# A hand-made instruction order for a transformer layer: its planner gets other durations, hand-over times and constants of choice

## The chip, the cores and the metric

The kernel runs on one core of one Trainium2 chip. A core has four engines that compute, each with its own instruction queue that is worked off in order: TensorE (PE in the profile; its weight loads are listed as PEld), VectorE (DVE), ScalarE (ACT) and GpSimd (POOL). SyncE (SP) issues DMA transfers. Engines wait for each other by semaphores. The metric is the device time of one execution in microseconds, the median of several runs.

## The reference

One layer of a transformer with pre-normalisation, on x of 2 x 2048 x 256 in float32: causal attention with 16 heads of 16 columns and rotary positions, then a gated feed-forward network of width 704 whose activations and weights are rounded to a 4-bit grid (FP4) in blocks of 16.

```python
def _L0_attn_ref(x, Wq, bq, Wk, bk, Wv, bv, Wo, bo):
    q = split_heads(x @ Wq.T + bq)
    k = split_heads(x @ Wk.T + bk)
    v = split_heads(x @ Wv.T + bv)
    q, k = (rope(q), rope(k))
    att = jnp.einsum('bhqd,bhkd->bhqk', q, k) / math.sqrt(HEAD_D)
    att = jnp.where(mask, att, -jnp.inf)          # lower triangle
    att = jax.nn.softmax(att, axis=-1)
    y = jnp.einsum('bhqk,bhkd->bhqd', att, v)
    return y.transpose(0, 2, 1, 3).reshape(b, t, N_EMBD) @ Wo.T + bo

def _L0_ffn_ref(x, w_gate, w_up, w_down):
    gate = fp4_linear(x, w_gate)                  # both operands through FP4
    y = fp4_linear(x, w_up)
    h = jax.nn.silu(gate) * y
    return fp4_linear(h, w_down)

x = L0_attn_x
x = x + _L0_attn_ref(_layernorm(x, axis=-1), ...)
x = x + _L0_ffn_ref(_layernorm(x, axis=-1), ...)
```

## The kernel before

**The work.** Each of the two sequences is cut into four chunks of 512 positions (c = 0 to 3), and the 16 heads into four groups of four. For a chunk and a group there are two passes over the keys up to the diagonal. The first computes scores with the queries on the partitions (`max_steps`, tile `sc`, line 900) and takes their row maxima on VectorE (line 924). The maxima are split into three bfloat16 parts (lines 958 and 961), transposed on TensorE (line 974) and copied to `mT` (line 980). The second pass (`value_steps`) computes scores with the keys on the partitions into tile `sx`: line 1017 puts minus the maximum there, line 1025 adds the product, line 869 the mask on the diagonal. ScalarE takes the exponential into `ex` (line 1040), and line 1070 multiplies it with the values into `av`. After the last key, `av` is copied, transposed and divided (lines 1092, 1104, 1114, 1118). Beside this run the projections of the next chunk (`project_steps`, `pj` line 701, `pv` line 819), the FP4 rounding of the weights (`weight_items`), and the output projection and feed-forward network of finished chunks (`ffn_steps`; `po` line 1225, `pg` line 1276, `pd` line 1359, transposes in line 1151).

**Three tilings.** TensorE is used in three ways: score products on two strips of 64 rows ("strip"), value products on column tiles of 32 ("value"), and everything else with the whole array ("whole").

**The order.** The program is straight-line, and its order on every engine is decided while it is built. Each step adds tasks to a `Plan` (lines 110 to 151) with `add(engine, cost, run, reads, writes, due, ...)`: `cost` is a duration in us that the programmer supplies, `due` a place on a scale of urgency. That scale (lines 1417 to 1427) gives each slot, a chunk and group, 0.4 (c+1) units for its first pass and 0.6 (c+1) for the second pass of the slot before, 80 units in all. `Plan.ordered` (lines 153 to 243) then plays the program through as a list scheduler: it keeps, for each engine, the time at which it is free, and for each task the time at which what it reads is ready. Again and again it takes the engine whose next task can start first, and among that engine's tasks that can start within PATIENCE of it the one with the smallest due. A task of TensorE with another tiling than the one before has CHANGE added to its due in that comparison, and pays ENTER in time once taken. Tasks due more than AHEAD after the oldest outstanding due aren't looked at. FEED_M and FEED_V are taken off the due of the score tasks, and TURN, in slots, puts off the second pass. HOP is the time from a task's end until a task on another engine can start on its result. Buffers are counted too: ROOM allows three `ps` tiles in PSUM (shared by `sc`, `sx`, `pj` and `pg`), four `ex` tiles, one `pm`, and so on; a task that needs a new one can't start before the last user of an old one has ended (`vacancy`, line 168). The order found is the order in which instructions are issued; the chip then runs them by semaphores, and the planned times have no other effect on it.

Of the kernel before, what the change touches and what calls it, by code (L numbers as in the profile page):

```python
# [66 lines left out]
AHEAD = 2.0  # L67
CHANGE = 0.02
FEED_M = 0.3
FEED_V = 0.3  # L70
PATIENCE = 0.15
TURN = 0.25
# [15 lines left out]
HOP = {PE: 0.235, DVE: 0.09, ACT: 0.09, POOL: 0.09, SP: 0.05}  # L88

ENTER = dict(strip=0.17, value=0.11, whole=0.12)  # L90
# [15 lines left out]
class Task:  # L106
    __slots__ = "engine cost run due tiling feeds left ready end after new".split()


class Plan:  # L110
# [7 lines left out]
    def add(  # L118
        self, engine, cost, run, reads=(), writes=(), due=0.0, books=(), tiling="whole", feeds=0.0
# [3 lines left out]
        t.tiling, t.feeds = tiling, feeds  # L123
# [29 lines left out]
    def ordered(self):  # L153
# [14 lines left out]
        def vacancy(kind):  # L168
# [5 lines left out]
            for thing in held:  # L174
                if all(u.end is not None for u in thing.users):
                    at = max(u.end + HOP[u.engine] for u in thing.users)
                    if best is None or at < best[0]:
                        best = at, thing
            return best

        while len(out) < len(self.tasks):
# [4 lines left out]
            for e, some in waiting.items():  # L186
# [3 lines left out]
                for due, n, t in some:  # L190
# [3 lines left out]
                    for thing in t.new:  # L194
                        if thing.kind not in vacant:
                            vacant[thing.kind] = vacancy(thing.kind)
# [23 lines left out]
            for thing in t.new:  # L220
                held = rooms[thing.kind]
                if len(held) == ROOM[thing.kind]:
                    held.remove(vacancy(thing.kind)[1])
# [13 lines left out]
            for a in t.after:  # L237
                a.left -= 1
                a.ready = max(a.ready, t.end + (HOP[e] if a.engine != e or e == SP else 0.0))
# [6 lines left out]
def on_scalar(n):  # L246
    return 0.2 + 0.833e-3 * n


def on_vector(n):  # L250
    return 0.178 + 1.042e-3 * n


def on_pool(n):
    return 0.12 + 2.3e-3 * n


def product(n):

    return max(n / 600, 0.28) + 0.01  # L260
# [7 lines left out]
def layer_kernel(  # L268
# [156 lines left out]
    def deviation(pool, kind, src, thing, due):  # L425
# [17 lines left out]
        add(DVE, 0.66, stats, [thing], [dev], due)  # L443
# [3 lines left out]
    def normed(dst, src, got, things, due):  # L447
# [4 lines left out]
        add(DVE, 0.46, run, *things, due)  # L452

    def fp4(src, thing, r, n, engine=POOL, step_of=None):
# [6 lines left out]
        by_block = 0.09 + 1.88e-3 * n if engine == POOL else on_vector(n)  # L461
# [7 lines left out]
        def scaled(due):  # L469
# [17 lines left out]
            add(DVE, on_vector(n) + 0.64, sizes, [thing], [small16], due)  # L487
            add(POOL, 0.24, nudged, [small16], [small16], due)
            add(engine, by_block, divided, [small16], [thing], due)

        def rounded(due):
# [24 lines left out]
            add(DVE, 2 * (0.18 + 0.55e-3 * n), powers, [thing], [step], due)  # L516
# [17 lines left out]
    def transpose_plain(raw, thing, put, target, due):  # L534
# [11 lines left out]
        add(PE, 0.57, turn, [thing, fixed], [pm], due)  # L546
# [9 lines left out]
    def load_rounded(w, row, rows, col, cols, put, target):  # L556
# [12 lines left out]
        def turn(due):  # L569
# [11 lines left out]
            add(PE, 0.3, run, [raw, fixed], [pm], due)  # L581
            add(ACT, 0.45, lambda: put(st["pt"]), [pm], [target], due)
# [39 lines left out]
    def norm_steps(b, c):  # L622
# [22 lines left out]
        def turn(i, due):  # L645
# [13 lines left out]
            add(PE, 0.3, run, [st[i]["in"], fixed], [pm], due, [xnT_[b, c]])  # L659
# [9 lines left out]
    def project_steps(b, c, blk):  # L669
# [22 lines left out]
        def product_of(i, due):  # L692
# [31 lines left out]
            add(ACT, on_scalar(CH), biased, [ps, bias_], [qb], due)  # L724
            add(DVE, on_vector(CH), cosines, [ps, cs_[b, c], bias_], [t1], due)

        def turned(i, due):
# [19 lines left out]
            add(DVE, 0.77, shuffled, [qb], [t2], due)  # L747
# [135 lines left out]
    def max_steps(b, c, g):  # L883
# [6 lines left out]
        def one(i, kc, d, due):  # L890
# [21 lines left out]
            def reduced():  # L912
# [15 lines left out]
                0.235 + 0.16 * (kc == c),  # L928
# [6 lines left out]
                FEED_M,  # L935
            )
            add(DVE, on_vector(2 * cols), reduced, [ps], [parts if c else mx], due)

        def split(due):
# [23 lines left out]
            if c:  # L963
                add(DVE, 1.3, run, [parts], [mx, left, slots_of], due - 0.1)
            else:
                add(DVE, 1.1, run, [mx], [left, slots_of], due - 0.1)

        def turn(due):
# [14 lines left out]
            add(PE, 0.57, run, [slots_of, fixed], [pm], due - 0.1, [max_[b, c, g]])  # L983
# [10 lines left out]
    def value_steps(b, c, g):  # L994
# [9 lines left out]
        def score(j, d, due):  # L1004
# [32 lines left out]
            def exponential():  # L1037
# [9 lines left out]
                0.235 + max(0.06, cols / 2400) + 0.02 + 0.16 * (j >= TPC * c),  # L1047
# [6 lines left out]
                FEED_V,  # L1054
            )
            add(ACT, on_scalar(2 * cols), exponential, [ps], [ex_[j, d]], due)

        def weigh(j, due):
            off = offset(j)

            def run():
# [18 lines left out]
                (CH - off) / 600 + 0.02,  # L1080
# [15 lines left out]
        def divide(due):  # L1096
# [31 lines left out]
            add(PE, 0.57, turn, [avs_, fixed], [pm], due, [rows_[b, c], den_])  # L1128
            add(DVE, 0.75, run, [pm], [rows_[b, c], den_], due)
# [12 lines left out]
    def transposed(src, n, source, dst, target, due):  # L1142
# [16 lines left out]
        add(PE, 0.02 + 0.137 * -(-n // P), turn, [source, fixed], [pm], due, [target])  # L1159
        add(ACT, on_scalar(full * P) + 0.3 * (rest > 0), put, [pm], [target], due)  # L1160
# [440 lines left out]
```

## Time and profile before

| | |
|---|---|
| median of 3 runs | 1509.29 us (1504.66 to 1509.73) |
| profiled execution | 1507.64 us, of which the span from first to last instruction 1505.7 |
| granted TensorE clock, mean | 0.954 |
| instructions | 26,420 |
| score products for the maximum (line 900) | 1280 matmuls, 286.4 us busy, 450 ns mean |
| score products for the exponential (lines 1017, 1025) | 1280 + 1280 matmuls, 235.6 and 330.6 us busy |
| value products (line 1070) | 2560 matmuls, 302.4 us busy |
| row maxima on VectorE (`parts`, line 924) | 576 reductions, 602.5 us busy, 1080 ns mean |
| exponentials on ScalarE (line 1040) | 640, 553.7 us busy, 896 ns mean |
| DMA | 72.29 MB, 19.0% of the time of the 16 DMA engines in the largest queue |

How to read it: the busy time of an engine is the union of its instructions' spans. Matmuls are pipelined, so that their spans overlap, and the time that a matmul costs the engine is seen better in the spacing of the starts. A group's idle time is the time that its engine stood still just before its instructions, put down to what ended that time.

### The profile page before, as it was taken

The page shows a single profiled execution, that of the slowest core. Times are in us where ns is not written, and L with a number is a line of the kernel's source. Part 1 is how long each engine was busy: PE and PEld are TensorE (multiplying, and loading weights), DVE is VectorE, ACT ScalarE, POOL GpSimd, SP SyncE. Part 2 cuts the span into 40 slices and gives each one's busy share as a digit, 9 for nine tenths or more (in the row PEclk, how much of TensorE's full clock was granted, in tenths as well). Part 3 has the DMA queues.
Part 4 walks back from the last instruction along what each step waited for, and adds up shares of the span by engine and source line. Part 5 has one row for each costly group of instructions (what it writes and reads, how often), then busy time and mean ns, then how long its engine had stood idle before and what let it go on. Part 6 is the DMA issues. An engine that isn't in the chain of part 4 may idle for free. (4 is left out here: it accounts for less than half of the span.)

```text
span 1505.7 us, 26420 instructions
## 1 busy us (share of the span) xinstructions
PE 1378.0 (92%) x10549; PEld 681.1 (45%) x10549; DVE 1068.2 (71%) x1720; ACT 716.0 (48%) x1022; POOL 526.0 (35%) x679
## 2 busy tenths in 40 slices
PE   4687899899999999999998999999999999999986
PEld 2344344444444444444355454544444444444344
DVE  2777767787678777775556877888778867775165
ACT  1332444455555455555644445444654455555711
POOL 4554533342233232232424434243332322222240
PEclk9588889999999999999999999999999999999978
DMA  4542412030120120120224312112120120000000
GB/s 126 130 114 41 109 56 50 15 95 18 50 51 8 46 61 25 47 50 8 67 56 103 86 29 77 27 50 64 48 49 8 53 46 12 8 11 8 5 0 14
DMA packets 48130, 72.29 MB, mean 48 GB/s; under 512 B 6660, under 2 KB 22408, under 8 KB 48008
## 3 DMA queue, kind: packets, MB, share of 16 engines
q1 hardware_dynamic: 47712, 70.35, 19.0%
q8 instruction: 83, 1.36, 0.4%
q10 hardware_dynamic: 296, 0.26, 0.1%
q14 instruction: 39, 0.32, 0.1%
HBM read 49.61 MB, written 20.97 MB: 47 GB/s over the span
## 5 line engine op out<-in xcount | busy, mean ns | idle before, releaser
L1040 ACT ACTIVATE ex<-sx 128x1024 f32<-128x1024 f32 (+3 forms) x640 | 553.7, 896 | 410.0 <-PE sx L1025 233.7
L924 DVE TENSOR_REDUCE parts<-sc 128x2 f32<-128x1024 f32 (+3 forms) x576 | 602.5, 1080 | 115.2 <-PE sc L900 67.4
L1025 PE MATMUL sx<-qT,kT 64*128 64x512 f32 (+3 forms) x1280 | 330.6, 530 | 0.0
L900 PE MATMUL sc<-kT,qT 64*128 64x512 f32 (+3 forms) x1280 | 286.4, 450 | 47.3 <-DVE parts L924 21.5
L1070 PE MATMUL av<-ex,v 128*32 128x512 f32 (+3 forms) x2560 | 302.4, 546 | 0.2 <-ACT ex L1040 0.2
L1017 PE MATMUL sx<-mT,less 64*128 64x512 bf16 (+3 forms) x1280 | 235.6, 359 | 26.6 <-DVE parts L924 12.0
L900 PEld LDWEIGHTS sc<-kT,qT 64*128 64x128 f32 x1280 | 128.9, 191 | 225.2 <-DVE parts L924 64.3
L482 POOL TENSOR_SCALAR inv<-inv 128x16 f32<-128x16 f32 (+2 forms) x82 | 17.6, 215 | 463.1 <-DVE inv L478 349.0
L1017 PEld LDWEIGHTS <-less 64*128 64x128 bf16 x1280 | 72.0, 94 | 189.7 <-issue 176.5
L1025 PEld LDWEIGHTS sx<-qT,kT 64*128 64x128 f32 x1280 | 131.9, 198 | 0.4
L1359 PE MATMUL pd<-wdT,hrT 128*128 128x256 f32 (+1 forms) x384 | 106.2, 413 | 2.2 <-ACT hrT L1157 2.0
L740 POOL TENSOR_TENSOR t<-t,cs 128x512 f32<-128x512 f32 x32 | 41.0, 1282 | 154.1 <-DVE t L734 146.6
L1070 PEld LDWEIGHTS av<-ex,v 128*32 128x32 f32 x2560 | 52.9, 108 | 76.1 <-issue 67.7
L1359 PEld LDWEIGHTS pd<-wdT,hrT 128*128 128x128 f32 (+1 forms) x384 | 69.3, 196 | 34.8 <-issue 19.0
L1276 PE MATMUL pg<-wuT,xT 128*128 128x352 f32 x224 | 75.3, 474 | 0.3 <-DVE parts L924 0.2
L440 POOL TENSOR_SCALAR ve<-mv 128x1 f32<-128x1 f32 x64 | 12.4, 193 | 181.1 <-DVE mv L436 178.0
L1276 PE MATMUL pg<-wgT,xT 128*128 128x352 f32 x224 | 74.4, 470 | 0.4 <-DVE parts L924 0.4
L701 PE MATMUL pj<-xnT,wqkT 128*128 128x512 f32 x128 | 69.5, 664 | 1.3 <-DVE parts L924 0.8
L711 ACT ACTIVATE qb<-pj,bqk 128x512 f32<-128x512 f32 x32 | 22.0, 688 | 92.1 <-DVE t L715 48.5
L869 PE MATMUL sc<-pick,mask_q 64*128 64x64 bf16 x1024 | 65.1, 201 | 0.0
L924 DVE TENSOR_REDUCE mx<-sc 128x2 f32<-128x256 f32 (+3 forms) x64 | 50.4, 812 | 19.1 <-PE sc L869 18.8
L1307 DVE SCALAR_TENSOR_TENSOR h<-pg,h 128x704 f32<-128x704 f32 x32 | 28.5, 890 | 48.4 <-PE pg L1276 48.2
(131 smaller groups left out, 1665.0 us busy)
## 6 DMA issues: line engine op xcount, KB each, us to landing
qT<-parts SPq DMA_DIRECT2D x128, 128.0 KB
kT<-parts SPq DMA_DIRECT2D x128, 128.0 KB
parts<-high SPq DMA_DIRECT2D x32, 256.0 KB
parts<-t SPq DMA_DIRECT2D x32, 256.0 KB
xin<-in_L_attn_x_dram SPq DMA_DIRECT2D x32, 128.0 KB
cs<-in_rope_dram SPq DMA_DIRECT2D x8, 512.0 KB
x<-in_L_attn_x_dram SPq DMA_DIRECT2D x28, 128.0 KB
out_dram<-x SPq DMA_DIRECT2D x28, 128.0 KB
```

The source lines that it names most:

```text
L701: nc.tensor.matmul(got["pj"], lhsT=wqkT[:, k, i, cols], rhs=xnTs[b, c][:, k, :], start=(k == 0), stop=(k == KE - 1),)
L740: nc.gpsimd.tensor_tensor(swapped, swapped, angles[b, c][:, 1, :], ALU.mult)
L869: nc.tensor.matmul(sc[:, h, col + at : col + at + STRIP], lhsT=strips(mask, h, half), rhs=strips(pick, h), start=False, stop=(half == 1),)
L900: nc.tensor.matmul(sc[:, h, :cols], lhsT=strips(qT, h, d, slice(i * P, (i + 1) * P)), rhs=strips(kT, h, duo, slice(0, cols)), start=True, ...
L924: nc.vector.tensor_reduce(dst, got[0][:, :, :cols], AX.X, ALU.max)
L1017: nc.tensor.matmul(sc[:, h, off:], lhsT=strips(less[d], h), rhs=strips(mT, h, slice(off, CH)), start=True, stop=False,)
L1025: nc.tensor.matmul(sc[:, h, off:], lhsT=strips(kT, h, duo, slice(jj, jj + P)), rhs=strips(qT, h, d, slice(off, CH)), start=False, stop=(j ...
L1040: nc.scalar.activation(ex[:, :, off:], got[0][:, :, off:], AF.Exp, scale=HD**-0.5)
L1070: nc.tensor.matmul(st["av"][SLOT * s : SLOT * (s + 1), off:], lhsT=v[:, at : at + SLOT], rhs=st[j, d][:, h, off:], start=(j == 0), stop=(j ...
L1276: nc.tensor.matmul(got["pg"][:, half, :IH], lhsT=split("xrT")[:, k, :], rhs=wT[:, k, half * IH : (half + 1) * IH], start=(k == 0), stop=(k ...
L1307: nc.vector.scalar_tensor_tensor(st["h"], got["pg"][:, :, :IH], 0.5, st["h"], ALU.mult, ALU.mult)
L1359: nc.tensor.matmul(st["pd"], lhsT=st["hrT"][:n, k, :], rhs=wdT[:n, k, :], start=(k == 0), stop=(k == KI - 1),)
```

## The change

It touches the planner and the figures given to it. What is computed, the instructions, the tiles and their numbers of buffers stay as they are; the order on all engines can come out differently. There are four parts.

1. The constants of choice AHEAD, CHANGE, FEED_M, FEED_V, PATIENCE and TURN get other values.
2. HOP becomes a table by engine of the producer and of the consumer, with an entry for the same engine too. A new field `late` of a task is a time after its end at which others see its result; its own engine is free before. ENTER gets smaller values.
3. The functions for durations (`on_scalar`, `on_vector`, `on_pool`, `product`) get other constants, and `turning(n)` is new, for n transposes.
4. The durations written at single tasks are replaced.

```diff
-AHEAD = 2.0
-CHANGE = 0.02
-FEED_M = 0.3
-FEED_V = 0.3
-PATIENCE = 0.15
-TURN = 0.25
+AHEAD = 1.5
+CHANGE = 0.04
+FEED_M = 0.1
+FEED_V = 0.4
+PATIENCE = 0.06
+TURN = 0.3
...
-HOP = {PE: 0.235, DVE: 0.09, ACT: 0.09, POOL: 0.09, SP: 0.05}
-
-ENTER = dict(strip=0.17, value=0.11, whole=0.12)
+HOP = {
+    PE: {PE: 0.0, DVE: 0.21, ACT: 0.21, POOL: 0.21, SP: 0.21},
+    DVE: {PE: 0.135, DVE: 0.12, ACT: 0.12, POOL: 0.17, SP: 0.17},
+    ACT: {PE: 0.155, DVE: 0.14, ACT: 0.14, POOL: 0.18, SP: 0.18},
+    POOL: {PE: 0.09, DVE: 0.075, ACT: 0.075, POOL: 0.12, SP: 0.12},
+    SP: {PE: 0.05, DVE: 0.05, ACT: 0.05, POOL: 0.05, SP: 0.05},
+}
+
+ENTER = dict(strip=0.11, value=0.08, whole=0.08)
...
-        def vacancy(kind):
+        def vacancy(kind, to):
...
-                    at = max(u.end + HOP[u.engine] for u in thing.users)
+                    at = max(u.end + u.late + HOP[u.engine][to] for u in thing.users)
...
             for a in t.after:
                 a.left -= 1
-                a.ready = max(a.ready, t.end + (HOP[e] if a.engine != e or e == SP else 0.0))
+                late = t.late if a.engine != e else 0.0
+                a.ready = max(a.ready, t.end + late + HOP[e][a.engine])
...
 def on_scalar(n):
-    return 0.2 + 0.833e-3 * n
+    return 0.066 + 0.833e-3 * n
 
 
 def on_vector(n):
-    return 0.178 + 1.042e-3 * n
+    return 0.065 + 1.042e-3 * n
 
 
 def on_pool(n):
-    return 0.12 + 2.3e-3 * n
+    return 0.14 + 2.14e-3 * n
 
 
 def product(n):
 
-    return max(n / 600, 0.28) + 0.01
+    return max(n / 600, 0.17 + n / 870, 0.23) + 0.005
+
+
+def turning(n):
+
+    return 0.01 + 0.13 * n
...
-        add(DVE, 0.66, stats, [thing], [dev], due)
+        add(DVE, 0.55, stats, [thing], [dev], due)
...
-        by_block = 0.09 + 1.88e-3 * n if engine == POOL else on_vector(n)
+        by_block = 0.14 + 1.71e-3 * n if engine == POOL else on_vector(n)
...
-            add(DVE, on_vector(n) + 0.64, sizes, [thing], [small16], due)
-            add(POOL, 0.24, nudged, [small16], [small16], due)
+            add(DVE, on_vector(n) + 0.36 + 0.005 * nb, sizes, [thing], [small16], due)
+            add(POOL, 0.17, nudged, [small16], [small16], due)
...
-            add(DVE, 2 * (0.18 + 0.55e-3 * n), powers, [thing], [step], due)
+            add(DVE, 0.263 + 1.033e-3 * n, powers, [thing], [step], due)
...
-        add(PE, 0.57, turn, [thing, fixed], [pm], due)
+        add(PE, turning(4), turn, [thing, fixed], [pm], due, late=0.05)
...
             add(
                 PE,
-                0.235 + 0.16 * (kc == c),
+                0.18 + 0.44e-3 * cols if kc == c else 0.27,
                 run,
                 [qT_[b, c, g], k_[b, kc, g // 2], fixed],
                 [ps, m_order],
@@
                 "strip",
                 FEED_M,
+                0.07,
             )
...
             if c:
-                add(DVE, 1.3, run, [parts], [mx, left, slots_of], due - 0.1)
+                add(DVE, 1.04, run, [parts], [mx, left, slots_of], due - 0.1)
             else:
-                add(DVE, 1.1, run, [mx], [left, slots_of], due - 0.1)
+                add(DVE, 0.79, run, [mx], [left, slots_of], due - 0.1)
...
             add(
                 PE,
-                0.235 + max(0.06, cols / 2400) + 0.02 + 0.16 * (j >= TPC * c),
+                0.455 if j < TPC * c else 0.14 + 0.75e-3 * cols,
                 run,
                 [qT_[b, c, g], k_[b, j // TPC, g // 2], max_[b, c, g], fixed],
                 [ps, e_order],
@@
                 "strip",
                 FEED_V,
+                0.22,
             )
...
             add(
                 PE,
-                (CH - off) / 600 + 0.02,
+                (CH - off) / 600 + 0.03,
                 run,
                 [ex_[j, 0], ex_[j, 1], v_[b, j // TPC, g // 2]],
```

The remaining lines of the diff replace durations of the same kinds: transposes by `turning(n)` with `late=0.05`, and single figures of ACT and DVE tasks in the projections, the division and the copies.

## The prediction, made before the changed kernel was seen

> **What bounds the kernel now.** I read the page from the top: busy shares, the forty slices, the costliest groups.
>
> ```profile
> span 1505.7 us, 26420 instructions
> PE 1378.0 (92%) x10549; PEld 681.1 (45%) x10549; DVE 1068.2 (71%) x1720; ACT 716.0 (48%) x1022; POOL 526.0 (35%) x679
> ...
> PE   4687899899999999999998999999999999999986
> ...
> PEclk9588889999999999999999999999999999999978
> ...
> PE 31%; DVE 10%; issue 3%; POOL 2%; ACT 1%; DMA 0%; ACTq 0%; POOLq 0%; DVEq 0%
> ```
>
> TensorE works in nearly every slice, and the chain of waits (it is followed back over about half the span) lies on PE three times as often as on VectorE. The stretches say where it is not so:
>
> ```profile
> 38.00:75.00 37.00, 26.03 (x215) 14.39 (x216) 26.80 (x55) 11.30 (x20) 19.31 (x29) 0.60 0.53 131
> 75.00:113.00 38.00, 30.71 (x288) 17.27 (x287) 27.98 (x63) 14.53 (x25) 21.32 (x31) 0.87 0.47 114
> ...
> 1204.00:1355.00 151.00, 147.45 (x1096) 68.60 (x1095) 109.84 (x152) 82.99 (x106) 38.85 (x47) 0.99 0.08 19
> ...
> 1430.00:1506.00 76.00, 56.76 (x172) 34.41 (x172) 46.74 (x86) 10.31 (x25) 16.94 (x33) 0.77 0.02 7
> ```
>
> Columns: stretch, length, busy time of PE, weight loads, DVE, ACT, POOL, granted clock, DMA share. Only the first 190 us and the last 76 us leave PE idle; between them a microsecond less on PE is nearly a microsecond less in all. But "busy" hides two costs that an order of work can change. The first is a change of tiling:
>
> ```profile
> 1084.26 0.99 PE av L1070 x8
> ...
> 1086.95 1.74 PE av L1070 x16
> ```
>
> These are pieces of the chain. Two value products in a row take 1.74, so 0.87 each; one that is followed by another tiling holds PE 0.99. Leaving costs 0.12 us. In the timeline of PE, start to start, a score product of 512 columns takes a median of 0.464 us before another (113 pairs) and 0.549 before a value product (91 pairs): 0.085. I take 0.1 us a change. Grouped into the list's tasks, the timeline has 2,131 PE tasks and 1,314 changes of tiling: 131 us, 8.7% of the span.
>
> The second cost is waits. For each kind of task and following tiling I took the spacing that a fifth of its pairs stay under and summed what the others have above it. From 190 to 1430 us that is 111 us: 241 events of 60 to 250 ns (29 us), 130 longer ones (77 us), the rest under 60 ns. Before 190 us it is 61 us, in the last two slices 14. Who ends such waits:
>
> ```profile
> PEld sc L900 <- DVE parts L924: 64.3, 97, 4.1
> ...
> PEld sc L900 <- ACT ex L1040: 40.7, 82, 1.1
> ...
> PE sc L900 <- DVE parts L924: 21.5, 36, 4.0
> ```
>
> A score product waits for a `ps` buffer, which the maximum (DVE) or the exponential (ACT) has yet to read.
>
> **The change part by part.** No instruction is added or removed; all sums below are changes of waiting and of order. Every task can move, on PE, DVE, ACT, POOL and on SP, whose some 560 DMA issues are tasks of the list too.
>
> *Durations and hops.* The list was made with figures that the trace contradicts. A maximum over 128x1024 is planned at 1.245 us; three in the chain take 3.39, 1.13 each, and the new figure is 1.132. An exponential is planned at 1.053; a pair takes 1.94 with 1.02 for one, so 0.92 each, new 0.919. A masked score product of 512 columns is planned at 0.628 and of 128 at 0.475; the median spacings are 0.52 and 0.254, new 0.524 and 0.236. Against that the hand-over from `sx` to ACT was 0.235 and becomes 0.21 + 0.22, DVE to PE 0.09 becomes 0.135, ACT to PE 0.09 becomes 0.155, and dependent work on one engine now has 0.12 to 0.14 where it had none. Filling, draining and freeing a `ps` buffer is thus 0.468+0.235+1.053+0.09 = 1.85 before and 0.455+0.43+0.919+0.155 = 1.96 after on the `sx` side: buffers were planned free 0.11 us too early. On the `sc` side it is 1.81 before and 1.82 after. The short waits have just the size of these errors and of PATIENCE, which let PE idle 0.15 us on purpose and now 0.06. Bounds for the 29 us: nothing gained, or all; I take half, **-15**, because where no other task is ready the wait stays whatever the list knows. The 130 long waits are larger than any hop error and come from drift between list and chip; bounds -40 (half) and +20 (a quarter more, a new order drifting elsewhere); I take a sixth, **-13**.
>
> *Tiling.* Entering a tiling falls in the plan from 0.17, 0.11, 0.12 to 0.11, 0.08, 0.08 (the trace: about 0.1), but this changes only the plan's time. What chooses is CHANGE, 0.02 to 0.04 in due units. The scale of dues has 80 units between the first score at 46.6 us and the last at about 1429, so one unit is about 17.3 us and 2,131 tasks lie 0.038 apart: the preference now reaches about one neighbour further. A smaller PATIENCE works against it, since fewer tasks compete. 640 of the 1,314 changes are the two ends of 320 value runs, of which 12 pairs merge now; so no more than a quarter can go, -33 us; +4 if patience wins. I take 6%, 80 times 0.1, **-8**.
>
> [...]
>
> *Feeds, TURN, AHEAD.* FEED_M falls from 0.3 to 0.1 and FEED_V rises from 0.3 to 0.4: scores for the maximum come 3.5 us later in due, those for the exponential 1.7 us earlier; TURN adds 0.05 of a slot. Between a slot's last maximum score and its first exponential the lead was 0.25 of a slot and is 0.3 of a slot less 0.3 units. In slots of one unit (c=0, eight of them) it falls from 4.3 us to nothing, in slots of four from 17 to 16. The path in that lead, a reduction, the split (1.21 in the chain), four transposes and a copy to `mT`, takes some 4 us. What covers it is other ready work: side tasks and the next slot's scores. Without that cover it is 8 x 4.3 = 34 us; waits of `sx` for `mT` are 2.0 us from 600 to 900 us now, so the cover is good: bounds 0 and +34, I take **+4**. Behind an `sx` that waits stand all PE tasks after it, and ACT waits for it. AHEAD from 2.0 to 1.5 lets side work run 26 us ahead and not 35; PE waited for a DMA 4.7 us in all, so late loads are not what costs now: 0, bounds 0 and +10.
>
> *Start and end.* Before 190 us the waits are single long ones (11.1 us of one transpose for `v`, 4.9 and 2.9 of scores for `high` and `kT`) that hang on chains through ACT, DVE and SP; an order can go either way there: **0**, bounds -15 and +15. The tail's dues are untouched and PE hands over to DVE and back: **0**, bounds 4 either way.
>
> Sum: -15 - 13 - 8 + 4 = -32 on the profiled execution's 1507.6 us (span and 1.9 around it): 1475.6. The median of the runs is 1.7 higher, so **1477**. The bounds taken as independent reach some 45 below and 40 above.
>
> **The rivals.** *A: same time, other order.* With three `ps` buffers each held about 1.9 us and 1,400 fillings, the rooms are held 2,660 of 3 x 1506 = 4,518 us; PE often has one candidate only, and better figures choose the same task or lose it elsewhere. For it: half of the long waits are for a buffer. Against it: half of the waits are no larger than the errors corrected. Time 1507, within 7.5.
>
> *B: slower by late maxima.* Scores for the maximum lose their head start, VectorE (71% busy, and 124 of 151 us from 903 to 1054) gets them in bunches, and `mT` comes after the `sx` that needs it. In its place the wait of `sx` for `mT` decides as soon as side work runs out, first in the c=0 slots, 45 to 130 and 750 to 820 us. Half of the 34 us uncovered is 17: 1526. If all is uncovered and nothing is gained, 1543. The granted clock of 0.60 from 38 to 75 us, where PE waited, would spread with it. Against it: the list still sees the wait and fills it with what is ready.
>
> *C: slower by the shorter horizon.* Weight preparation and projections, held back to 26 us ahead, meet their due time late; the front of 61 us of waits grows by a quarter, 15 us: 1522. Against it: the dues of that work are early already and the horizon binds only what runs ahead.
>
> **How the numbers follow.** What a measurement here can tell from no change is 0.5%, 7.5 us. The forecast, 1477 (its own range 1445 to 1500): 0.66. A: 0.15. B: 0.12. C: 0.07. Faster takes the forecast and a few hundredths of A that fall outside; slower B, C and as much: 0.67, 0.13, 0.20. The range takes in the forecast's lower bound and reaches to B and C's near ends: 1445 to 1523.
>
> **What would show it.** Changes of tiling counted in the timeline near 1,235; the 60 to 250 ns waits near half; the two weight-load waits of `sc` together under 85 us; PE's busy time lower, since changes of tiling lie inside it, and its share near 93%. Wrong it is if `sx` waits for `mT` over 15 us (B), if PE idle before 190 us grows by more than 10 us (C), or if counts and waits both stand still (A).

## The result and the profile after

The changed kernel takes 1512.43 us (median of 14 runs, 1509.28 to 1516.87); the kernel before, beside it, 1505.76 us (14 runs, 1500.47 to 1513.86). The ratio is 1.0037, with an interval from 1.0021 to 1.0054: not faster, and probably a little slower, by less than the 0.5% that the prediction set as its bound. The profiled execution took 1513.34 us, its span is 1511.6, its granted clock 0.953, against 1507.64, 1505.7 and 0.954.

The page of the changed kernel, the same lines as of before (and VectorE's slices):

```profile
span 1511.6 us, 26408 instructions
...
PE 1369.9 (91%) x10549; PEld 688.5 (46%) x10549; DVE 1087.4 (72%) x1720; ACT 716.5 (47%) x1022; POOL 525.7 (35%) x679
...
PE   4698899899999899999998999989999899999986
...
DVE  2778778777877787766566777788687868776165
...
PEclk9588899899999899999999899999999989999988
...
PE 60%; DVE 26%; issue 5%; POOL 4%; ACT 4%; DMA 1%; SPq 0%; ACTq 0%; POOLq 0%; DVEq 0%
```

TensorE has 8 us less work and the span is 6 us longer, so it stands still 14 us more. And VectorE is busy 19 us longer (1068.2 before) with the same 1720 instructions: some of them have become slower, which the prediction did not expect of a new order. The same stretches as before:

```profile
38.00:75.00 37.00, 22.61 (x142) 13.24 (x142) 27.24 (x57) 8.61 (x16) 22.86 (x36) 0.55 0.70 158
75.00:113.00 38.00, 34.80 (x380) 18.77 (x378) 27.27 (x57) 17.49 (x31) 17.39 (x24) 0.88 0.30 82
1204.00:1355.00 151.00, 142.50 (x1052) 68.70 (x1056) 116.32 (x160) 77.02 (x99) 41.62 (x50) 0.97 0.08 19
1430.00:1506.00 76.00, 59.95 (x262) 36.80 (x257) 46.12 (x86) 14.57 (x35) 17.14 (x33) 0.83 0.02 7
```

The loss isn't at the start but in the middle: from 1204 to 1355 us TensorE's work falls from 147.45 to 142.50 of 151, and VectorE's rises from 109.84 to 116.32. By the ends of the chunks the changed kernel is 11.5 us ahead after the first three (the last `sx` of chunk 2 at 497.5 us from the first `sc`'s 47.5, against 508.1 from 46.6), and gives back 16 in the five that follow. The waits of score products:

```profile
PEld sc L915 <- DVE parts L939: 55.8, 88, 2.1
PEld sc L915 <- ACT ex L1065: 39.9, 72, 1.1
PE sc L915 <- DVE parts L939: 23.9, 38, 2.0
PE sx L1042 <- DVE parts L939: 22.9, 33, 2.1
```

(Columns: us in total, times, longest.) The first three sum to 119.6, before 126.5. The fourth is new among the large ones; in the kernel before it was

```profile
PE sx L1017 <- DVE parts L924: 12.0, 22, 1.1
```

It is the same wait for a `ps` buffer that a maximum still reads, now in front of the second pass.

**Where VectorE's 19 us went.** One group shows it best, the normalising `xn` (28 instructions over 128x256, one after each `rstd` of GpSimd). By operation and shape, columns: count, busy us, mean ns, idle before; first before, then after:

```profile
L450 DVE TENSOR_SCALAR xn<-x,mv,rstd 128x256 f32<-128x256 f32 x28 | 13.4, 477 | 6.1 <-POOL rstd L441 6.0
```

```profile
L463 DVE TENSOR_SCALAR xn<-x,mv,rstd 128x256 f32<-128x256 f32 x28 | 25.4, 908 | 4.6 <-POOL rstd L454 4.4
```

The same instruction takes twice as long. The timeline shows what goes with it, here at one place near the end. Columns: start, length, engine, line, operation. GpSimd in the changed kernel:

```profile
1382.45 1.70 POOL L523 TENSOR_TENSOR h<-h,step 128x704 f32<-128x704 f32 x1
1384.23 0.19 POOL L453 TENSOR_SCALAR ve<-mv 128x1 f32<-128x1 f32 x1
1384.50 0.55 POOL L454 TENSOR_TENSOR rstd<-ve,minus_half 128x1 f32<-128x1 f32 x1
1385.02 1.39 POOL L526 TENSOR_TENSOR h<-h,scale 128x704 f32<-128x704 f32 x1
```

VectorE there:

```profile
1385.09 1.47 DVE L463 TENSOR_SCALAR xn<-x,mv,rstd 128x256 f32<-128x256 f32 x1
1386.48 1.21 DVE L939 TENSOR_REDUCE parts<-sc 128x2 f32<-128x1024 f32 x1
```

and TensorE:

```profile
1386.11 1.06 PE L1096 MATMUL av<-ex,v 128*32 128x512 f32 x8
1387.75 0.34 PE L1042 MATMUL sx<-mT,less 64*128 64x384 bf16 x2 [0.58 <-DVE parts L939]
```

`rstd` ends at 1385.05 and frees two things at once: `xn` on VectorE, and on GpSimd's own queue the next pass over `h`. `xn` starts 0.07 us behind that pass, ends at 1386.56, 0.15 after the pass does (1386.41), and has taken 1.47 us for work of 0.405. The maximum behind it ends at 1387.69, and TensorE has waited 0.58 us for the buffer that it frees. The same place in the kernel before, GpSimd and then VectorE:

```profile
1373.16 1.70 POOL L510 TENSOR_TENSOR h<-h,step 128x704 f32<-128x704 f32 x1
1374.93 1.39 POOL L513 TENSOR_TENSOR h<-h,scale 128x704 f32<-128x704 f32 x1
1379.65 0.19 POOL L440 TENSOR_SCALAR ve<-mv 128x1 f32<-128x1 f32 x1 [3.33 <-DVE mv L436]
1379.92 0.55 POOL L441 TENSOR_TENSOR rstd<-ve,minus_half 128x1 f32<-128x1 f32 x1
```

```profile
1380.51 0.41 DVE L450 TENSOR_SCALAR xn<-x,mv,rstd 128x256 f32<-128x256 f32 x1 [0.95 <-POOL rstd L441]
```

There the three passes over `h` are done before `ve`, GpSimd has nothing behind `rstd`, and `xn` takes 0.41.

I call this the clash. It holds for every `xn` of the trace: 20 of the 28 `xn` of the changed kernel begin while a GpSimd instruction runs, and each of the 20 ends 0.147 to 0.153 us after that instruction; the other 8 take 0.404 to 0.409. Before, 4 of 28 begin so. The place to look is GpSimd's queue: another pass follows `rstd` at once in 12 of 28 cases, before in 1. Other instructions that are held so are tensor-scalar and some tensor-tensor instructions from SBUF to SBUF at float32 or int32: of those of the changed kernel that begin under a GpSimd instruction, 14 of 17 `xin`, 13 of 17 `scale`, 24 of 33 `step` and 17 of 22 `mslots` exceed their group's lower quartile by over 0.08 us, and before 3 of 3 `left`. The reductions for `scale` (20 begin so in the changed kernel), the reciprocals (21) and the statistics for the normalising (52) never do, though some of them also read and write SBUF; nor do the maxima, which read PSUM (217 `parts` begin under a GpSimd instruction before and 164 after, and none is longer than the others). **Stretch** from here on is the time by which VectorE's instructions exceed the lower quartile of those with the same operation, output tile and shape, summed over those that exceed it by more than some 0.08 us: 30.9 us in 57 instructions before and 57.8 in 96 after. The difference, 26.9 us, is nearly that of the summed durations of all 1720 instructions (1128.8 and 1155.3 us, 26.5 apart); the busy time grew by less, since it is a union and spans overlap.

In the trace `xn` is held until GpSimd's whole running instruction has ended, up to 1.32 us here; by what, it doesn't show. It happens the other way too, with less effect: a pass of GpSimd that begins while VectorE's `xin` runs takes 0.84 us, where the median of this pass is 0.73.

```profile
331.16 0.41 DVE L463 TENSOR_SCALAR xin<-xin,mv,rstd 128x256 f32<-128x256 f32 x1
```

```profile
331.32 0.84 POOL L520 TENSOR_TENSOR xn<-xn,step 128x256 f32<-128x256 f32 x1 [0.56 <-DVE step L517]
```

### The profile page after: what moved, and what is told of

Same layout as the page of the kernel before. It is cut to its first block, busy times and chain, and to the rows that moved or that the text cites. A ratio compares the mean times of both kernels' runs of the same rounds, so it can differ in the third digit from the quotient of the medians.

```text
span 1511.6 us, 26408 instructions
## 1 busy us (share of the span) xinstructions
PE 1369.9 (91%) x10549; PEld 688.5 (46%) x10549; DVE 1087.4 (72%) x1720; ACT 716.5 (47%) x1022; POOL 525.7 (35%) x679
## 4 chain that ended last, share of the span: by engine, by line
PE 60%; DVE 26%; issue 5%; POOL 4%; ACT 4%; DMA 1%; SPq 0%; ACTq 0%; POOLq 0%; DVEq 0%
PE av L1096 13%; DVE parts L939 11%; PE pg L1320 10%; PE sc L915 7%; PE sx L1042 7%; PE sx L1050 6%; PE pd L1403 5%; PE pj L716 3%; PE pth L1186 2%; ACT ex L1065 2%; PE pv L834 2%; DVE scale L487 1%; DVE xn L463 1%; DVE mx L939 1%; DVE step L514 1%
## 5 line engine op out<-in xcount | busy, mean ns | idle before, releaser
L939 DVE TENSOR_REDUCE parts<-sc 128x2 f32<-128x1024 f32 (+3 forms) x576 | 609.4, 1080 | 144.3 <-PE sc L915 101.5
L915 PE MATMUL sc<-kT,qT 64*128 64x512 f32 (+3 forms) x1280 | 274.4, 439 | 46.1 <-DVE parts L939 23.9
L939 DVE TENSOR_REDUCE mx<-sc 128x2 f32<-128x1024 f32 (+3 forms) x64 | 50.4, 813 | 20.2 <-PE sc L884 20.1
L1343 ACT ACTIVATE h<-pg 128x704 f32<-128x704 f32 x32 | 24.3, 758 | 83.1 <-PE pg L1320 74.9
L520 POOL TENSOR_TENSOR h<-h,step 128x704 f32<-128x704 f32 x28 | 47.2, 1685 | 46.0 <-DVE step L517 43.5
```

The lines of the kernel that those rows point to most:

```text
L520: queue.tensor_tensor(src(), src(), st["step"], ALU.add)
L915: nc.tensor.matmul(sc[:, h, :cols], lhsT=strips(qT, h, d, slice(i * P, (i + 1) * P)), rhs=strips(kT, h, duo, slice(0, cols)), start=True, ...
L939: nc.vector.tensor_reduce(dst, got[0][:, :, :cols], AX.X, ALU.max)
```

## The experiments

Theory **P**: the new durations are worth having, and the new constants of choice produce an order in which the clash doubles and takes the gain back. Rivals: **C**, the new constants are bad by themselves; **S**, the old figures were too long and so left slack, which the new ones take away; **R**, the order has gained nothing to begin with, any new order moves the time a little, and the clash is incidental. A table first, the single experiments below it. Clock is the median granted clock of the runs; stretch and PE waits (spacing of starts above the lower-fifth spacing of that kind of task and following tiling) are those of the one profiled execution, and another grouping that keeps shapes apart shifts a row of PE waits by some 10 us and a difference of two rows by some 6; changes of tiling are counted in the list itself. The kernel before was run again with each batch of experiments; its medians lie between 1505.1 and 1506.8 us, and the ratios are to the one of the same batch. Times go with the clock, by 0.87 us for 0.001 (last section), so a difference between two kernels at unlike clocks may be partly that: of the 6.7 us of the change up to 4.3.

| kernel | median us (runs) | ratio to before [interval] | clock | stretch us | PE waits us | changes |
|---|---|---|---|---|---|---|
| before | 1505.76 (14) | | 0.957 | 30.9 | 249.6 | 1268 |
| changed | 1512.43 (14) | 1.0037 [1.0021, 1.0054] | 0.952 | 57.8 | 259.1 | 1238 |
| changed, old constants | 1490.98 (6) | 0.9912 [0.9884, 0.9941] | 0.9625 | 33.2 | 233.7 | 1257 |
| before, new constants | 1502.23 (13) | 0.9978 [0.9960, 0.9995] | 0.958 | 30.0 | 232.7 | 1224 |
| before, GpSimd cut | 1472.59 (6) | 0.9768 [0.9742, 0.9794] | 0.9645 | 1.4 | 215.3 | 1268 |
| changed, GpSimd cut | 1469.83 (6) | 0.9752 [0.9725, 0.9778] | 0.964 | 1.7 | 215.3 | 1238 |
| changed, clash planned at `normed` | 1505.91 (12) | 0.9996 [0.9979, 1.0014] | 0.953 | 42.0 | 251.6 | 1233 |
| changed, clash planned | 1500.37 (12) | 0.9959 [0.9943, 0.9975] | 0.952 | 39.2 | 243.9 | 1217 |
| same, `sc` at 0.34 | 1490.44 (5) | 0.9900 [0.9874, 0.9926] | 0.960 | 35.2 | 236.8 | 1249 |
| changed, PATIENCE 0.15 | 1497.01 (10) | 0.9942 [0.9920, 0.9964] | 0.9575 | 37.1 | 237.5 | 1231 |
| changed, old feeds and TURN | 1522.91 (6) | 1.0109 [1.0077, 1.0140] | 0.955 | 62.1 | 265.3 | 1271 |
| changed, AHEAD 2.0 | 1514.92 (12) | 1.0058 [1.0036, 1.0080] | 0.955 | 45.3 | 256.1 | 1250 |
| before, PATIENCE 0.06 | 1502.78 (12) | 0.9985 [0.9965, 1.0004] | 0.9605 | 34.6 | 241.7 | 1278 |
| changed, GpSimd cut, PATIENCE 0.15 | 1472.31 (6) | 0.9772 [0.9742, 0.9803] | 0.965 | 1.4 | 208.5 | 1231 |
| changed, GpSimd cut, old constants | 1465.59 (6) | 0.9733 [0.9695, 0.9771] | 0.9675 | 1.6 | 215.0 | 1257 |
| all together, CHANGE 0.3 | 1483.64 (5) | 0.9844 [0.9819, 0.9869] | 0.955 | 22.0 | 226.6 | 1141 |
| all together, CHANGE 0.02 | 1478.44 (6) | 0.9826 [0.9789, 0.9864] | 0.9645 | 30.1 | 216.7 | 1271 |

### The parts of the change alone

The changed kernel with the six constants set back ("this clash" in the expectation is the one described above):

```diff
-AHEAD = 1.5
-CHANGE = 0.04
-FEED_M = 0.1
-FEED_V = 0.4
-PATIENCE = 0.06
-TURN = 0.3
+AHEAD = 2.0
+CHANGE = 0.02
+FEED_M = 0.3
+FEED_V = 0.3
+PATIENCE = 0.15
+TURN = 0.25
```

> The changed kernel with the six constants of choice set back (AHEAD 2.0, CHANGE 0.02, FEED_M 0.3, FEED_V 0.3, PATIENCE 0.15, TURN 0.25); the new durations, hand-over times and tiling figures stay. [...] Theory P (the planner doesn't know of this clash, and the new order has more of it): this list has a stretch near that of before, 30 to 40 us, and with figures closer to the trace it is faster than before by 0.4 to 1.2%, 1488 to 1500 us. Theory S (the old figures were too long and so left slack, which the new ones take away): 1508 to 1520 us, as the changed kernel, with waits of TensorE as large. Theory C (the constants of choice do the harm): 1490 to 1502 us, but with a stretch that doesn't matter either way. Theory R (any other order moves the time by some 0.5% at random): anywhere from 1498 to 1515.

The reverse of the same diff on the kernel before:

> The kernel before with the six new constants of choice alone; durations, hand-over times and tiling figures as before. Theory P: the stretch stays near that of before (30 to 40 us), little is won by 44 fewer changes of tiling (1,224 for 1,268, 4 us) and something lost by scores for the maximum that come later: 1500 to 1512 us. Theory S: the slack is still there, so no slower than before: 1498 to 1508. Theory C: slower than before by as much as the changed kernel or more, 1510 to 1522. Theory R: 1498 to 1515.

The durations and hops alone make the kernel 0.9% faster, 1490.98, with the stretch at 33.2, almost that of before; by the slope of the clock 4.8 of these 14.8 us may go with it (0.9625 against 0.957). S, which wanted 1508 to 1520 here, falls. The constants alone do next to nothing, 1502.23, stretch 30.0, and C falls. (The profiled execution of that kernel was the fastest of its 13, at 1490.05, so its 232.7 us of waits are below its usual ones.) The loss is in the pair: with the new durations the constants cost 21.4 us, with the old ones they bring 3.5.

### The clash taken away

In both kernels GpSimd's long passes (FP4 passes, rotary products, the bias on `x`) run on 16 columns only; the other columns are left out, so the times are of a kernel with less work on GpSimd. The order of each stays as it was.

```diff
+        def few(queue, dst, a, b, op):
+            n1 = 1 if queue is nc.gpsimd else nb
+            queue.tensor_tensor(dst[:, :n1, :], a[:, :n1, :], b[:, :n1, :], op)
...
-                queue.tensor_tensor(src(), src(), st["step"], ALU.add)
+                few(queue, blocks(src()), blocks(src()), blocks(st["step"]), ALU.add)
...
-                nc.gpsimd.tensor_tensor(swapped, swapped, angles[b, c][:, 1, :], ALU.mult)
+                nc.gpsimd.tensor_tensor(
+                    swapped[:, :BLOCK], swapped[:, :BLOCK], angles[b, c][:, 1, :BLOCK], ALU.mult
+                )
```

The order before:

> The kernel before with its own order kept instruction by instruction, but GpSimd's long passes (the FP4 scaling and rounding, the rotary products and sums, the bias of the output projection) work on 16 columns in place of 256 to 704; so these parts are left out for the other columns. This takes the clash away: VectorE's stretch falls from 30.9 us to under 5. It is one half of a pair with the changed order under the same cut. Theory P: about 20 to 35 us faster than before, 1470 to 1488 us, partly by shorter chains through GpSimd. Theories S, C and R: the same, since they say nothing of GpSimd.

The changed order:

> The changed order, kept instruction by instruction, under the same cut of GpSimd's passes to 16 columns; these parts are left out for the other columns. Theory P: the changed order was slowed by 27 us more of stretching, so without GpSimd's passes it comes out ahead of the order of before under the same cut, by 8 to 25 us (ratio 0.983 to 0.995), although with them it is 6 us behind. Theory S and theory C: it stays behind, by 0 to 10 us, since slack and choice are as they were. Theory R: within 8 us either way.

The group of `xn` in the changed order with cut passes:

```profile
L463 DVE TENSOR_SCALAR xn<-x,mv,rstd 128x256 f32<-128x256 f32 x28 | 11.3, 404 | 1.3 <-POOL rstd L454 1.3
```

404 ns on average (396 to 415), and stretch of 1.7 us in all. From 6.7 us behind, the changed order comes to 2.8 ahead: a swing of 9.5 us. The direction is P's, but P wanted 8 to 25 us ahead and its number is missed; 2.8 us lies within the spread of the runs, and R, with its 8 us either way, got its range here. So this pair shows that the changed order is no longer behind, and no more. PE waits, 9.5 us apart with whole passes, are 215.3 each.

### The planner knows the clash

The list scheduler is given what the trace shows: an instruction with the mark `port` that would begin while a GpSimd task runs is planned to begin when that task ends.

```diff
+        pool = 0.0, 0.0
...
                     at = max(t.ready, free[e])
+                    if t.port is not None and pool[0] < at + t.port < pool[1] - 0.1:
+                        at = pool[1] - t.port
...
+            if e == POOL:
+                pool = at, at + t.cost
...
-        add(DVE, 0.33, run, *things, due)
+        add(DVE, 0.33, run, *things, due, port=0.0)
```

The last line, the normalising, is the only one marked in the first kernel; in the second the FP4 steps (`sizes`, `powers`) and the split of the maxima are marked as well.

> The changed kernel with the clash known to the planner for one kind of task alone, the normalising in front of the FP4 rounding and of the projections, which has 14.1 + 7.3 us of the stretch after and 2.0 + 6.0 before. Theory P: the stretch falls to 40 to 48 us and the time to 1499 to 1508 us, about half of what the full knowledge gave (1500.4). Theory S, C and R: 1507 to 1517.

The second kernel:

> [...] Theory P: VectorE's stretch falls from 57.7 us to under 30, the waits of TensorE for buffers that VectorE empties fall by 10 to 20 us, and the time is 1487 to 1502 us, faster than the changed kernel by 0.7 to 1.7% and faster than before. Theory S and theory C: the stretch falls but TensorE's waits don't, 1507 to 1517 us. Theory R: 1500 to 1517.

Marked at the normalising alone, the mean of `xn` falls from 908 ns to 525 and the time by 6.5 us; marked everywhere, by 12.1 us, at the same clock as the changed kernel (0.952). So an order that avoids part of the clash brings 12 us with all other figures and constants of the change in place. It avoids part only: stretch is 39.2 and not the under 30 that I expected, since list and chip drift apart (`mslots` 11.1 and `scale` 10.1 us remain).

One more wrong figure drives that drift: an unmasked `sc` is planned at 0.27 us and its median spacing is 0.339, 384 times, 27 us.

```diff
-                0.18 + 0.44e-3 * cols if kc == c else 0.27,
+                0.18 + 0.44e-3 * cols if kc == c else 0.34,
```

> As the run with the clash known to the planner, and the one duration that is still far from the trace is set right: an unmasked score product for the maximum at 0.34 us and not 0.27 (the median spacing is 0.339 between two strips). Theory P with the thought that a truer figure helps: 1482 to 1498 us, a few us under the run without it. Theory S (slack helps, and 0.34 gives the plan 27 us of it): clearly faster than the run without it, by over 10 us. Theory R: the two differ by less than 8 us in either direction.

1490.44, 9.9 us less than without. The clock is 0.960 against 0.952, though, and by the slope at the end of this document 7 of the 10 us may go with that; PE waits fall by 7.1. What the figure itself is worth stays unclear.

### Which constant

PATIENCE back to 0.15, then FEED_M, FEED_V and TURN back, then AHEAD back, each in the changed kernel:

```diff
-PATIENCE = 0.06
+PATIENCE = 0.15
```

> The changed kernel with PATIENCE alone set back to 0.15. Question: which constant of choice brings the clash of VectorE and GpSimd that the six old constants (together) take away. Theory P1 (PATIENCE: with 0.06 an engine takes what can start at once, and so the list packs GpSimd's passes right against the normalising instructions): the stretch of VectorE's instructions falls from 58 us to 30-40 and the time to 1492-1503, most of the way to the 1491 of all six. Theory P2 (the lead of the scores, FEED_M, FEED_V, TURN): stretch stays above 50 and time 1507-1515.

```diff
-FEED_M = 0.1
-FEED_V = 0.4
-TURN = 0.3
+FEED_M = 0.3
+FEED_V = 0.3
+TURN = 0.25
```

> The changed kernel with FEED_M and FEED_V set back to 0.3 and TURN to 0.25. Theory P1 (PATIENCE): stretch stays at 50-65 us, time 1505-1515; the wait of sx for parts (22.9 us in the changed kernel) stays above 18. Theory P2 (the lead): the wait of sx for parts returns to about 12 us, stretch to 30-40, time to 1492-1503.

```diff
-AHEAD = 1.5
+AHEAD = 2.0
```

> The changed kernel with AHEAD alone set back to 2.0. P1 and P2: little, 1505-1515, stretch 45-60. Theory P3 (the horizon: with 1.5 the side work, whose normalising and FP4 passes meet GpSimd, is pushed closer together): stretch 30-42 and 1495-1505.

It is PATIENCE: 1497.01, 15.4 of the 21.4 us of all six (some 5 of them and 9 of the 21.4 may go with the clock), and the stretch falls to 37.1. The group of `xn` and the wait of `sx` in that kernel:

```profile
L463 DVE TENSOR_SCALAR xn<-x,mv,rstd 128x256 f32<-128x256 f32 x28 | 14.2, 507 | 4.1 <-POOL rstd L454 4.1
```

```profile
PE sx L1042 <- DVE parts L939: 11.9, 19, 1.7
```

Both are back near the kernel before (477 ns; 12.0 us). At the place shown above GpSimd's queue has `h<-h,scale` ahead of `ve` and `rstd` again:

```profile
1365.63 1.70 POOL L523 TENSOR_TENSOR h<-h,step 128x704 f32<-128x704 f32 x1
1367.41 1.39 POOL L526 TENSOR_TENSOR h<-h,scale 128x704 f32<-128x704 f32 x1
1368.88 0.19 POOL L453 TENSOR_SCALAR ve<-mv 128x1 f32<-128x1 f32 x1
1369.15 0.55 POOL L454 TENSOR_TENSOR rstd<-ve,minus_half 128x1 f32<-128x1 f32 x1
```

Why a small PATIENCE puts `ve` and `rstd` between two passes can be read from the planner. In its new table GpSimd hands over to itself in 0.12 us; before, the next task of the same engine was ready at once. The list looks only at tasks that can start within PATIENCE of the first. With 0.15 the next pass over `h` is among them; with 0.06 it isn't, and whatever is ready at that moment goes first. On the chip's GpSimd the last pass of the rounding (`scale`) stands directly behind the pass before it in 50 of 78 cases in the changed kernel, in 77 before, in 77 with PATIENCE or all six constants back, and in 75 with PATIENCE 0.06 in the kernel before. So it takes both, the new hop and the small PATIENCE. (Played through with 0.05 in place of that 0.12, the list of the changed kernel has 76 of 78; such a kernel was not run.) The planner itself can't see the harm: its own end of the list is 1445.6 us for the changed kernel and 1459.0 with PATIENCE back, 13 us in favour of what costs 15 on the chip.

With the feeds and TURN set back, the kernel got 10.5 us slower than the changed one, where I expected 1505 to 1515: at this PATIENCE those three new constants help. AHEAD does little in time (2.5 us slower); the stretch fell to 45.3 without any gain, so the sum of stretch alone doesn't give the time.

### Does PATIENCE cost through GpSimd's passes, or by its order?

The cut of above on the changed kernel with PATIENCE back, and on the one with all six back; then PATIENCE 0.06 alone in the kernel before. Q in the expectations is the rival that the order of a small PATIENCE is worse in itself.

> The changed kernel with PATIENCE back at 0.15 and GpSimd's long passes on 16 columns, as in the earlier pair with cut passes (changed order: 1469.8 us, order before: 1472.6). With whole passes PATIENCE alone is worth 15.4 us (1512.4 against 1497.0). Theory P (PATIENCE costs through the collision of VectorE with GpSimd): without the passes its worth shrinks under 5 us, 1465-1475. Theory Q (the order that a small PATIENCE makes is worse in itself): at least 8 us of the 15 stay, 1453-1462.

> The changed kernel with all six constants of choice set back and GpSimd's long passes on 16 columns. With whole passes the six are worth 21.4 us (1512.4 against 1491.0). P: without the passes less than 7 us, 1463-1475. Q: at least 11 of the 21 stay, 1448-1459. The worth of the new durations with the old constants, without the passes: P leaves 0-9 us against the order before (1472.6), Q 14 and more.

> The kernel before with PATIENCE alone at 0.06. Q (a small PATIENCE is worse with any durations): 1512-1525. P: it costs only where GpSimd's passes come to lie against VectorE's instructions; with the old durations (all six new constants left the stretch at 30 us) the stretch stays at 25-36 us and the time at 1496-1510.

With passes cut short, PATIENCE back at 0.15 brings nothing (1472.31 against 1469.83), where it brought 15.4; all six bring 4.2, where they brought 21.4. Q falls in both. In the kernel before, PATIENCE at 0.06 costs nothing either (1502.78, interval 0.9965 to 1.0004, stretch 34.6). So, as far as these runs go, PATIENCE costs only together with the new durations and hops and only while GpSimd's passes are long. One reservation: the cut takes away the clash and at once shortens what GpSimd's own consumers wait for; but those waits weren't longer in the changed kernel (VectorE for `rstd` ahead of `xn` 4.4 us, before 6.0; ahead of `xin` 6.3, before 10.8; TensorE's weight loads for the last pass over `h` 2.3, before 3.7), so the clash is the part that differs.

The same runs set a bound on the other side. Without the passes the best order with the new durations is 7.0 us ahead of the order before (1465.59 and 1472.59, at clocks of 0.9675 and 0.9645): in this kernel without a clash the new figures aren't worth the 28 us of waits that I gave them.

### All together

The planned clash, `sc` at 0.34 and the old constants, with CHANGE at 0.3 and at 0.02:

> What the runs so far point to, together: new durations and hand-over times, the unmasked score product at 0.34 us, the clash known to the planner, and the constants of choice of before except CHANGE, which is 0.3 and leaves 1,141 changes of tiling for 1,268. Theory P, with fewer changes of tiling at 0.1 us each: stretch under 35 us, 1475 to 1490 us, the fastest so far. Theory R: 1485 to 1505.

> The fastest version so far (new durations, the planner knows of the clash, score products of 512 columns at 0.34, old constants of choice, CHANGE 0.3: 1483.6 us, 1,141 changes of tiling) with CHANGE back at the old 0.02: about 1,260 changes, so some 120 more. If a change of tiling costs the 0.1 us that the prediction used and none of it is given back, 1493-1499. If fewer changes are paid for by waits elsewhere, 1481-1488. Stretch 20-25 us in both.

Both beat both kernels; against the one before by 1.6% and 1.7%. `xn` is at 407 ns in each of the two, and stretch is 22.0 and 30.1, the second above what I expected. The 130 changes of tiling that CHANGE 0.3 saves bring nothing that shows: PE waits are 9.9 us higher, and the time 5.2, and 1478.44 lies under both ranges that I had stated for CHANGE 0.02. As the clocks differ (0.955 and 0.9645), which is better isn't settled; but 13 us from 130 changes at 0.1 it is not.

Taken together, the table speaks against R. Over the ten kernels with the new durations and whole passes, time and stretch go together with a correlation of 0.92, 1.1 us of time for 1 us of stretch (0.9 when the clock is allowed for by its slope); the three with the old durations lie 9 to 16 us above that line. It isn't a law: AHEAD 2.0 lies 10 us above it.

## Why the prediction was wrong

**The bound** was read rightly: TensorE sets the end, its busy time fell by 8.1 us, and its waits decided.

**Durations and hops, -28 of waits** (-15 short, -13 long): this step failed. Counted in the same way, the 60 to 250 ns waits went from 29.9 to 27.5 us, and the longer ones between 190 and 1430 us from some 75 to 93, at the bad end of the bounds (+20). All waits of the list's spacing rose by 9.5 us, 12.4 of them in front of `sx`. Two things in the step's argument were wrong. I counted the smaller PATIENCE as part of the gain ("which let PE idle 0.15 us on purpose and now 0.06"), but it holds for every engine, GpSimd too. I had noted that dependent work on one engine now has 0.12 to 0.14 us, and not that this is more than 0.06 and less than 0.15: so the list broke up GpSimd's chains, and setting PATIENCE back alone is worth 15.4 us. And I took a VectorE instruction's duration as a constant that the planner had now got right, when the trace of before held 30.9 us of stretch in instructions with up to nearly seven times their usual length (a `scale` of 0.17 us took 1.18); the group of `xn` had 477 ns with most at 405. In the changed kernel the stretch is 57.8 us, 26.9 more. With the old constants the durations brought 15.9 us of waits and 14.8 us of time: half of what I took, the right sign.

**Tiling, -8**: right in sign, too large. The list has 1,268 changes before and 1,238 after; my 1,314 came from grouping starts, which counted some twice. 30 fewer at 0.1 are 3 us; TensorE's spacing without waits fell by 3.7. I had 80 fewer. That the count of 1,238 meets the forecast's 1,235 is luck, since both the start and the saving were wrong.

**Feeds and TURN, +4**: no sign of it. `sx` waits for `mT` 1.7 us, before 3.3, and setting the feeds back made the kernel slower, not faster.

**AHEAD, start, end, 0**: right. AHEAD alone set back changed 2.5 us. TensorE's work in the first 190 us rose from 135.07 to 140.16, so its idle time there fell by 5 and the first chunk was 5.4 us shorter; from the last `sx` to the end it is 77.8 us, before 77.3.

**The rivals.** A came nearest, same time with another order (1507, within 7.5), but for another reason: the order did change for the better and the clash took it back. B's sign, a wait of `sx` for `mT` over 15 us, isn't there (1.7); what did rise was the wait of `sx` for a buffer that a maximum still read, which I hadn't named. C's sign isn't there. Of the marks set beforehand, the changes near 1,235 (1,238, by luck) and the lower PE busy time came; the two weight-load waits of `sc` together are 95.7 and not under 85, and PE's share is 91%, not 93%. The bounds were also added up wrongly: taken as independent, those stated reach 52 us above the forecast and not 40, so the forecast's own range, up to 1500, was too narrow on that side.

**What stays open.** Up to 4 of the 6.7 us may go with the clock (0.952 against 0.957), though the two profiled executions differ by 5.9 us at 0.953 and 0.954. How the loss divides between instructions that wait out a pass and passes that come later because `ve` and `rstd` stand between them was not measured: the planned clash brought 12.1 us while the last pass still stood directly behind the one before in only 60 of 78 cases.

## What to carry to other kernels

Before better durations are put into a hand-made schedule, look for instructions whose duration isn't one number: a group whose mean stands well above its minimum (`xn`, 477 ns against 401) tells of something that the schedule doesn't know; here the 4 `xn` that began under a GpSimd instruction took 0.72 to 1.04 us and the other 24 at most 0.41. A sharper schedule can meet it more often (20 of 28 after the change, stretch 57.8 us for 30.9) and lose more by it than better figures bring; a constant that looks like slack may be what keeps the two apart, as PATIENCE 0.15 did here (stretch 37.1, 15.4 us). Compare such a constant with the hand-over times too: a PATIENCE below the hop within an engine lets other work in between the parts of a chain there. Change figures and constants of choice in separate steps: here one half was worth 0.9% and the two together less than nothing.

## What the runs showed of the hardware

- The normalising `xn` on VectorE (128x256 float32 from SBUF to SBUF, 0.405 us) ends 0.15 us after GpSimd's instruction where it begins while one runs: 20 of 20 in the changed kernel, up to 1.47 us long. The other side is held less: with lines and shapes kept apart, GpSimd's own stretch is some 2 us before and 3 after. In the changed kernel a pass of it that begins while one of VectorE's tensor-scalar instructions runs is longer by up to 0.17 us (0.89 for 0.73 at 1466.48 us); one that begins under the tensor-tensor `h` takes 1.24 for 0.72 (1465.16 us), and a `rstd` under which a `step` of VectorE begins 0.92 for 0.55 (450.81 us).
- The time of one and the same program goes with the granted clock of its run. Over 23 runs of the kernel before the correlation is -0.89 and 0.001 of mean clock goes with 0.87 us; 14 runs of the changed kernel show the same slope, and three other batches of the kernel before 0.99 to 1.16. That the lower clock is the cause, and not the mark, of a slower run wasn't tested; in forty equal windows of the changed kernel's profile it is lowest from 38 to 151 us (0.55, 0.89, 0.83) and from 1436 us on (0.82, 0.81), where TensorE is busy 23.2, 34.6, 30.5, 30.4 and 26.0 of 37.8 us; three other windows have 0.86 (from 264, 491 and 831 us, with 33.7, 32.2 and 35.3 us busy), two 0.90 (from 151 and 1209 us, with 33.2 and 37.1), and the rest 0.93 or more.
- A change of tiling costs 0.085 to 0.12 us in the kernel before, as the spacing of single tasks shows it (0.549 us for 0.464, 0.99 for 0.87), yet 130 fewer of them (all together, CHANGE 0.3 against 0.02) lowered TensorE's spacing without waits by only 2 to 4 us, depending on how the tasks are grouped.
